# A graph layer on one core: where the norm roots run, when small loads and columns are made, and another order of the edge stage

## The chip, the core and the metric

The kernel runs on one core of a Trainium2 chip. The metric is device time in microseconds (us) of one execution. Five engines work side by side, each on its own in-order list of instructions: TensorE (PE, matrix products), VectorE (DVE), ScalarE (ACT), GpSimd (POOL, which here also issues the indirect loads, called gathers) and SyncE (SP, which issues most of the other transfers). Where one needs another's result it waits on a semaphore.

## The reference: what is computed

625 nodes with 512 values each, 20625 edges (a source, a destination, one of four types and a weight; the last 625 are loops of a node to itself). Cut to what matters:

```python
h = relu(layernorm(x))
total = sum over r of (h[src] @ W_rel[r] + b_rel[r]) * where(edge_type == r, edge_weight, 0)
agg   = segment_sum(total, dst) / maximum(segment_sum(edge_weight, dst), 1)
h2    = h @ W_self + b_self + agg
x1    = layer_norm(h + h2, g1, b1)
ffn   = gelu(x1 @ W_ffn1 + b_ffn1) @ W_ffn2 + b_ffn2
out   = x + layer_norm(x1 + ffn, g2, b2)
```

All is float32. Every layer norm needs one reciprocal square root for each node: this is the "root" of the text.

## The kernel before, in words

The nodes stand in 5 blocks of 125, the edges in 162 tiles of 128. The work has two stages, and the order of the instructions of every engine is fixed when the program is written: in the first stage by the order of the Python lines, in the second by a planner.

**Table stage.** x is loaded by block (`load_x`) and normalised without its root: `x_stats` (L346, L348) takes the statistics, `pre_norm` subtracts the mean and cuts at zero on DVE (L336, L337) and has POOL make the root as a power of -0.5 (`rsqrt_pow`, L313). PE turns each block (L320). Then come 20 steps, for relation r = 0 to 3 and block i = 0 to 4: `table_rows(r, i)` multiplies block i by W_rel[r] (L367), ACT scales the rows by the root (L375), and SP writes them to a table in DRAM (L377); the last nine stay in SBUF as well. A step is four matmuls; the profile shows two steps, 8 matmuls, as 3.49 us where nothing disturbs them.

Between these steps the Python lines put the work that prepares the edges. It is a chain:
- `find_tiles` (L467 to L470, DVE) searches `first_of_tile`, a row with the first destination of each tile, that SP loads at L221; `rows_of_tiles` has POOL gather five rows of destinations (L463, `dst`).
- `find_windows` (L477 to L482, DVE) searches these, and POOL gathers five windows of edges (L463, `win`).
- `edge_columns` (L423 to L427, DVE) makes columns of all edges, from `ed`, with no part in the chain.
- `slot_weights` and `slot_fields` (L494 to L523, DVE) turn the windows to fields; PE turns the fields (`turn_fields`, L598).
- `slot_hots` (L615, L618, L621, DVE) makes one-hot vectors of a quarter of a block's slots (a unit); `slot_sums` (L632, PE) multiplies them into a PSUM bank, and `empty_sums` (L638, DVE) adds three parts of it up to `sums_w`. There are 12 units for the three "dense" blocks 0 to 2; the first six are made in the table stage, the others in the edge stage.
- `first_edges` gathers, for each of the two other blocks, the first edges (L556). `first_columns` (L562 to L574, 13 short DVE steps) makes columns of them, and is the planner's `first_ready`.

SP's loads stand in the program's order too: x, W_rel[0], `first_of_tile` (between x's third block and the fourth and fifth), the edges, W_rel[1], and, by `later_loads(r)` after each relation, W_rel[2] and [3], W_self, `rows` (six rows of 512 values, each broadcast to 128 partitions, 1.5 MB, L210) and the weights of the feed-forward part. `rows` holds b_self, g1, b1, g2, b2 and b_ffn2 in this order.

**Edge stage.** A class `Plan` simulates the engines with a cost for each step, a `lag` after which a result is taken as there, counts of buffers (8 gathered tiles `ms`, three chunks `tr`, four PSUM banks `ps` and single ones for sums), and a rank or level for choosing between steps that could start. The order that it finds is emitted as each engine's order; the simulation's times are not used otherwise. Its steps:
- For each block the self part: 8 matmuls (L387) and a DVE step to z (L391).
- Blocks 0 to 2 (dense): 20 chunks of table rows times `sums_w` (L1044). The nine kept tiles are read from SBUF, the eleven others loaded by two with a lag of 6.2 (`chunk_load`, L1039).
- Blocks 3 and 4 by edges: 69 gathers of table rows on POOL (L920, by threes, with a pair of short pauses L916 after every fourth) with a lag `LAND` of 3.0. In each of 23 units ACT scales the first tile (L926), DVE adds the two others (L944), and PE sums the unit into its nodes with a one-hot matrix (L952). For a unit that is `parted`, ACT and DVE split the rows in a high and a low half (L930, L934) and PE runs two short matmuls (L964, L965); for one that is not, PE runs a full float32 product (L967). Of each list of units the last three are not parted. `gather_first` (L974) and `add_first` (L970) add single edges that cross a boundary, four gathers in all.
- When a block's sums are complete, its first norm: statistics and mean on DVE (L669, L300, L303/L305), the root, `za` (L676), x1 (L680), z = x1 + b_ffn2 (L683). The root is eight short DVE steps (`rsqrt_steps`: L651, L652, then L657 and L658 three times); for block 4 it is POOL's power (L313).
- Feed-forward of the block: PE (L715), gelu on ACT (L719), PE (L733), DVE (L741); then the second norm in the same way (L744, L300, L305, the root, L751, L756) and the store (L782). The blocks go in the order 0, 1, 3, 2, 4. The last one runs in two parts, and its root is ACT's square root with one DVE correction.
- `shifted`: xs + b2 for each block on DVE (L908), when nothing more urgent is there.

```python
if engine == "PE":
    o.lag = max(lag, Plan.BEHIND)
o.after = [(a, a.us if order and a.engine == engine else a.us + (0.0 if a.engine == engine == "PE" else a.lag))
           for a in after if a is not None]
```

These lines say when a step may start in the plan: after every step that it needs, plus that step's lag; nothing for a PE step behind a PE step.

Of the kernel before, what the change touches and what calls it, by code (L numbers as in the profile page):

```python
# [16 lines left out]
P = 128  # L17
# [51 lines left out]
class Plan:  # L69
# [5 lines left out]
    BEHIND = 1.0  # L75

# [60 lines left out]
def gnn_layer(ctx, tc, x, edges, edge_groups, firsts, fourths, windows, w_self, w_rel, w_ffn1, w_ffn2, brel_in, rows_in, bf1_in, out, n_edges):  # L137
# [74 lines left out]

    first_of_tile = early.tile([P, NT], I32, name="first_of_tile")
# [26 lines left out]
    bself_bc, g1_bc, b1_bc, g2_bc, b2_bc, bf2_bc = (  # L240
        rows[:, i * D:(i + 1) * D] for i in range(6))
# [68 lines left out]
    def rsqrt_pow(t):  # L310

        v, y = t[:, 0:1], t[:, 1:2]
        nc.gpsimd.tensor_tensor(y, v, half, op=ALU.pow)  # L313
        return y
# [348 lines left out]

    def first_norm(zi, name, got, pool_pow=False):
# [40 lines left out]
    def feed_forward(x1T_b, box, members, name, halves=False):  # L705
# [15 lines left out]
        def down(i):  # L721
# [24 lines left out]
            def mean_():  # L746
                got["mean"], got["t"] = aggregate(got["st"][:n, :len(cols), :], f"y{name}_{i}")
# [25 lines left out]
            norm.append(("scaled", "DVE", 0.72, scaled, ["a", "r3", "x"]))  # L773
# [16 lines left out]
    LAND = 3.0  # L790
# [15 lines left out]
    with tc.manual_schedule(engines={PE, DVE, ACT, mybir.EngineType.Pool}):  # L806
# [86 lines left out]
    first_ready = op("DVE", 2.4, first_columns, rank=(0.3,), level=6)  # L893

# [10 lines left out]

    shifted = {}
    for n, b in enumerate(ep.order):
        shifted[b] = op("DVE", 0.69, lambda b=b: nc.vector.tensor_add(xs[:, b, :], xs[:, b, :], b2_bc),  # L908
                        after=[own[b]], rank=(0.9, n), level=7)
# [26 lines left out]
    def parted(k, units):  # L936
        return k % PARTED[1] < PARTED[0] and k + 3 < len(units)
# [47 lines left out]
    for bs, units_ in of_sum.items():  # L985
        m, k0 = None, 0
        for b in inner:
            if bs == ((b, b + 1) if b < inner[-1] else (b,)):
                for q in range(EG - 1):
                    g_last = op("POOL", GATHER, lambda b=b, q=q: gather_first(b, q, ms), after=[g_last, first_ready],  # L990
# [59 lines left out]
    def weights_of(d):  # L1050
        nonlocal h, e
        for i, (dd, u) in enumerate(units):
# [3 lines left out]
            free = m[OUTER[d - 2]] if d >= 2 and u == 0 else None  # L1056
            h = op("DVE", 2.9, lambda d=d, u=u, box=box: box.update(hots=slot_hots(d, u)), after=[h], take=["low"],
                   rank=(0.55, i), level=0.18)
            for q in range(UNIT // QT):
                mm = op("PE", 0.33, lambda d=d, u=u, q=q, box=box: box.update(p=slot_sums(d, u, q, *box["hots"], (ps, "ps"))),  # L1060
                        after=[h, e, free], take=["ps"], give=["low"] if q == UNIT // QT - 1 else [], lag=0.25,
                        rank=(2, 1 + 0.01 * i), level=0.55)
                e = op("DVE", 0.57, lambda d=d, u=u, q=q, box=box: empty_sums(d, u, q, box["p"]), after=[mm], give=["ps"],
# [231 lines left out]
```

## Time and profile before

| | |
|---|---|
| median of 3 runs | 275.99 us (274.05 to 277.57) |
| the profiled execution | 278.13 us |
| its span, first to last instruction | 276.3 us |
| granted TensorE clock, mean | 0.977 |
| stages in the profile | table stage to about 91 us, edge stage from there |
| transfers | 47.94 MB, mean 173 GB/s |

How to read the lines that follow in the prediction. A group line has the line in the code, engine, operation, output <- inputs, shapes and count; then busy us and mean ns of one, then the idle time of the engine just before these instructions and what ended it. A timeline line has start, length, engine, line and operation, and in brackets the idle time before and its releaser. A waits line names who waited for what: us in total, times, longest. A chain line belongs to the chain of work that ended last. PEclk is the granted clock in tenths for 40 equal slices of the span (6.9 us each), 9 being 90% or more. Ends of matmuls are modelled and overlap the next one's start. L numbers in this document are those of the kernel before, unless it is said otherwise.

### The profile page before, as it was taken

How to read it: one execution, taken by the hardware profiler on the slowest of the kernel's cores; microseconds unless marked ns; L12 is line 12 of the kernel's file. 1: busy time of each engine (PE TensorE's matmuls, PEld its weight loads, DVE VectorE, ACT ScalarE, POOL GpSimd, SP SyncE). 2: the span in 40 equal slices, each digit the busy share in tenths (PEclk: the TensorE clock that was granted, in tenths of full speed). 3: DMA queues.
4: the chain of work that ended last, by engine and by line, in shares of the span. 5: the costliest groups of instructions: out<-in, count | busy, mean ns of one | idle time of the engine just before them, and what ended most of it. 6: DMA issues, size and time to landing. Idle time of an engine off the chain costs nothing.

```text
span 276.3 us, 3214 instructions
## 1 busy us (share of the span) xinstructions
PE 254.9 (92%) x1047; PEld 142.6 (52%) x1047; DVE 190.6 (69%) x447; ACT 63.9 (23%) x122; POOL 103.5 (37%) x148
## 2 busy tenths in 40 slices
PE   7999994999999997997896997899999999999990
PEld 3444441454554543453442456755367659494960
DVE  5540517989996859987899797799974976060614
ACT  3231112011310203221321022333044204030320
POOL 6252330002200067767775867574767010000000
PEclk9999997799999999999999899999999999999998
DMA  6939859466312577589999996563689101010101
GB/s 226 313 125 320 302 184 370 184 188 242 94 61 64 155 216 202 161 248 297 278 316 296 278 284 193 129 177 89 182 240 314 47 1 39 0 37 0 38 4 41
DMA packets 19972, 47.94 MB, mean 173 GB/s; under 512 B 2351, under 2 KB 3065, under 8 KB 19824
## 3 DMA queue, kind: packets, MB, share of 16 engines
q1 hardware_dynamic: 13348, 27.54, 30.5%
q0 software_dynamic: 6304, 19.89, 24.6%
q10 hardware_dynamic: 300, 0.26, 0.3%
q8 instruction: 9, 0.15, 0.2%
q14 instruction: 11, 0.09, 0.1%
HBM read 41.29 MB, written 6.52 MB: 173 GB/s over the span
## 4 chain that ended last, share of the span: by engine, by line
PE 62%; DMA 12%; POOL 8%; issue 8%; DVE 6%; SPq 1%; ACT 0%; DVEq 0%; POOLq 0%
PE pt L367 14%; PE pu L715 13%; PE po L733 12%; PE acc L1044 12%; POOL ms L920 5%; DMA tr<-table 5%; PE bank L632 3%; DMA ms<-table,row_i 3%; DMA xs<-in_x_dram 3%; PE acc L967 3%; DMA win<-in_windows_dram,at_i 2%; POOL dst L463 2%; PE pz L387 1%; PE acc L965 1%; PE acc L964 1%
## 5 line engine op out<-in xcount | busy, mean ns | idle before, releaser
L920 POOL DMA_INDIRECT ms<-table,row_i x69 | 69.3, 1004 | 55.7 <-DMA tr<-table 27.1
L367 PE MATMUL pt<-wr,hT 128*128 128x512 f32 x160 | 74.3, 614 | 0.0
L367 PEld LDWEIGHTS pt<-wr,hT 128*128 128x128 f32 x160 | 30.4, 197 | 33.5 <-issue 32.9
L715 PEld LDWEIGHTS pu<-x1T,w_sb 128*128 128x128 f32 x320 | 37.5, 192 | 5.2 <-issue 5.1
L715 PE MATMUL pu<-x1T,w_sb 128*128 128x125 f32 x320 | 38.0, 275 | 1.1 <-issue 1.1
L1044 PE MATMUL acc<-tr,sums_w 126*128 126x512 f32 x66 | 33.1, 626 | 3.4 <-DMA tr<-table 2.6
L733 PE MATMUL po<-w_sb,gT 128*125 128x512 f32 (+2 forms) x96 | 36.0, 522 | 0.0
L638 DVE TENSOR_REDUCE sums_w<-bank 126x160 f32<-126x480 f32 x48 | 29.9, 649 | 7.5 <-PE bank L632 6.7
L944 DVE SCALAR_TENSOR_TENSOR ea<-ms,wgt_g,ea 128x512 f32<-128x512 f32 x38 | 27.9, 747 | 10.4 <-DMA ms<-table,row_i 4.1
L926 ACT ACTIVATE ea<-ms,ed 128x512 f32<-128x512 f32 x23 | 15.8, 690 | 56.7 <-DMA ms<-table,row_i 27.9
L375 ACT ACTIVATE m<-pt,rx 125x512 f32<-125x512 f32 x20 | 13.8, 688 | 56.8 <-PE pt L367 45.2
L632 PEld LDWEIGHTS <-low 128*128 128x128 bf16 x192 | 17.2, 147 | 18.1 <-issue 17.8
L719 ACT ACTIVATE gT<-pu,bf 128x125 f32<-128x125 f32 x40 | 14.6, 367 | 49.6 <-PE pu L715 44.8
L1044 PE MATMUL acc<-m,sums_w 126*128 126x512 f32 x54 | 25.3, 597 | 0.0
L733 PEld LDWEIGHTS po<-w_sb,gT 128*125 128x125 f32 x96 | 16.3, 188 | 14.2 <-issue 12.1
L741 DVE TENSOR_TENSOR y<-po,z 125x512 f32<-125x512 f32 (+2 forms) x6 | 3.6, 601 | 26.3 <-PE po L733 26.3
L1044 PEld LDWEIGHTS acc<-tr,sums_w 126*128 126x128 f32 x66 | 12.2, 198 | 14.9 <-issue 11.0
L632 PE MATMUL bank<-high,low 128*128 128x120 bf16 x192 | 17.5, 226 | 2.4 <-issue 1.3
L387 PE MATMUL pz<-ws_sb,hT 128*128 128x512 f32 x40 | 18.1, 596 | 0.0
L621 DVE TENSOR_TENSOR high<-eq,turned 128x640 bf16<-128x640 bf16 x36 | 15.5, 487 | 0.4
L615 DVE TENSOR_TENSOR low<-turned,grid 128x2000 bf16<-128x2000 bf16 x12 | 14.3, 1190 | 1.3 <-ACT turned L601 1.3
L1044 PEld LDWEIGHTS acc<-m,sums_w 126*128 126x128 f32 x54 | 9.7, 191 | 8.9 <-issue 8.8
(169 smaller groups left out, 232.3 us busy)
## 6 DMA issues: line engine op xcount, KB each, us to landing
tr<-table SPq DMA_DIRECT2D x15, 504.0 KB
table<-m SPq DMA_DIRECT2D x20, 250.0 KB
w_sb<-in_L_gnn_W_ffn_dram SPq DMA_DIRECT2D x2, 2048.0 KB
wr<-in_L_gnn_W_rel_dram SPq DMA_DIRECT2D x3, 1024.0 KB
rows<-in_rows_dram SPq DMA_DIRECT2D x1, 1536.0 KB
ms<-table,row_i POOLq DMA_INDIRECT x69
ws_sb<-in_L_gnn_W_self_dram SPq DMA_DIRECT2D x1, 1024.0 KB
out_dram<-y SPq DMA_DIRECT2D x4, 224.0 KB
```

The lines of the kernel that those rows point to most:

```text
L367: nc.tensor.matmul(p, hT[i][:, k, :], wr_sb[r][:, k, :], start=(k == 0), stop=(k == KD - 1))
L387: nc.tensor.matmul(p[0], hT[i][:, k, :], ws_sb[:, k, :], start=(k == 0), stop=(k == KD - 1))
L621: nc.vector.tensor_mul(high[:, :, a * 2 * NC:(a + 1) * 2 * NC, :], eq, pairs(2 + a))
L632: nc.tensor.matmul(p[:, i * W:(i + 1) * W], low[:, t // TB, :, t % TB], high[:, t // TP, :, t % TP], start=True, stop=True)
L638: nc.vector.tensor_reduce(sums_w[OUTER[d]][:NG + 1, :, n0:n0 + 2 * QT].rearrange("p c (t h) -> p t h c", h=2), p[:NG + 1, :QT * 3 * 2 * NC ...
L715: nc.tensor.matmul(pu[:, :nn], w1_sb[:, k, f * P:(f + 1) * P], x1T_b()[:, k, :nn], start=(k == 0), stop=(k == KD - 1))
L719: nc.scalar.activation(box["gT"][:, f, :nn], pus[f][:, :nn], AF.Gelu, bias=bf1[:, f:f + 1])
L733: nc.tensor.matmul(po[h][:n, :w], box["gT"][:, f, at], w2_sb[:, f, c], start=(f == 0), stop=(f == KF - 1))
L920: nc.gpsimd.indirect_dma_start(out=ms[j], out_offset=None, in_=table[:, :], in_offset=bass.IndirectOffsetOnAxis(ap=row_i[:, j:j + 1], axis=0))
L926: nc.scalar.activation(box["sum"], ms[j], AF.Copy, scale=wgt[:, j:j + 1])
L944: nc.vector.scalar_tensor_tensor(to, ms[j], wgt_g[:, k, q - 1:q], box["sum"], op0=ALU.mult, op1=ALU.add)
L1044: nc.tensor.matmul(acc[b,], sums_w[b][:NG + 1, c, :], kept[(b, c) if (b, c) in kept else c][:NG + 1], start=first, stop=last)
```

## The change

- Roots: `root_by_pool` makes the root as one power on POOL in all first norms (block 4 had it so) and in the second norms of all blocks but the last one in order: eight norms move. The root waits in the plan for its mean with a lag, has cost 0.6 and goes ahead of all other POOL steps that could start (level -1).
- Loads: `first_of_tile` is loaded before x's third block instead of after it. `rows` is loaded in three parts: b2 alone (256 KB) right after W_rel[1], the first four rows (1 MB) and the last (256 KB) where the whole was loaded.
- Table stage: in the step (0, 0), `find_tiles` comes between the norm of x's third block and the statistics of its fourth; the roots of the fourth and fifth block come between the gathers. The five additions of b2 (`shifted` of before) stand in step (1, 0) after `edge_columns`. `first_columns` stands in step (3, 2). `first_ready` and `shifted` are gone from the plan.
- Plan: a PE step that follows DVE or ACT is planned 1.5 later, a POOL step 0.8 later. `LAND` is 4.5, the lag of a chunk load 8.0. The last unit alone of each list is not parted (before: the last three): of the 23 units 20 are split instead of 15. Slot sums of a unit do not wait for the emptying of the sums before; all units of the third dense block wait for the end of the first one's sum (before: the first unit of it). Levels of some DVE steps change; the second dense block takes the kept tiles first as the others do.

The plan's order therefore changes throughout the edge stage. For each engine the number of instructions in the list goes from 651 to 654 on PE, from 490 to 428 on DVE, from 154 to 159 on ACT, from 146 to 156 on POOL and from 93 to 95 on SP. In the new order of PE, the slot sums of the last two units of the second dense block stand right after the start of the second self part, the first edge sum comes after some 25 us of PE work of the stage (before: some 15), and all slot sums of the third dense block come before the first feed-forward product.

```diff
     BEHIND = 1.0
+    AFTER = {"PE": 1.5, "POOL": 0.8}
...
-        o.after = [(a, a.us if order and a.engine == engine else a.us + (0.0 if a.engine == engine == "PE" else a.lag))
-                   for a in after if a is not None]
+        behind = Plan.AFTER.get(engine, 0.0)
+        o.after = [(a, a.us if order and a.engine == engine else a.us + (0.0 if a.engine == engine == "PE" else a.lag)
+                    + (behind if a.engine in ("DVE", "ACT") and a.engine != engine else 0.0)) for a in after if a is not None]
...
     load_wr(0, [(2, 4)])
+    nc.sync.dma_start(first_of_tile, bass.AP(tensor=firsts.tensor, offset=firsts.offset, ap=[[0, P], [1, NT]]))
     load_x(2, 3)
-    nc.sync.dma_start(first_of_tile, bass.AP(tensor=firsts.tensor, offset=firsts.offset, ap=[[0, P], [1, NT]]))
     load_x(3, NB)
     nc.sync.dma_start(ed, edges)
     load_wr(1)
+    load_rows(b2_bc, 4 * D, 5 * D)
...
-            load_rows(rows, 0, 6 * D)
+            load_rows(rows[:, :4 * D], 0, 4 * D)
+            load_rows(rows[:, 5 * D:], 5 * D, 6 * D)
...
+    def root_by_pool(box, first):
+        return [("r3", "POOL", 0.6, lambda: rsqrt_pow(box["t"]), [first])]
...
-        rs = [("r3", "POOL", 0.9, lambda: rsqrt_pow(got["t"]), ["mean"])] if pool_pow else \
-            rsqrt_steps(got, "mean")
+        rs = root_by_pool(got, "mean") if pool_pow else rsqrt_steps(got, "mean")
...
-            norm += [] if halves else rsqrt_steps(got, "mean")
+            if not halves:
+                norm += root_by_pool(got, "mean") if pool_pow else rsqrt_steps(got, "mean")
...
-    LAND = 3.0
+    LAND = 4.5
...
-                    next_norm(i + 2 if i == 0 else i + 3)
+                    if i == 0:
+                        nonlocal stats
+                        pre_norm(2, stats)
+                        find_tiles()
+                        stats = x_stats(3)
+                    else:
+                        next_norm(i + 3)
...
-                if r == 0 and i < 3:
-                    if i == 0:
-                        next_norm(3)
-                        find_tiles()
-                    rows_of_tiles(2 * i, min(2 * i + 2, NB))
+                if (r, i) == (0, 0):
+                    rows_of_tiles(0, 2)
+                    next_norm(3)
+                    rows_of_tiles(2, 4)
+                if (r, i) == (0, 1):
+                    rows_of_tiles(4, NB)
...
                     edge_columns()
+                    for n in range(NB):
+                        nc.vector.tensor_add(xs[:, n, :], xs[:, n, :], b2_bc)
...
+                if (r, i) == (3, 2):
+                    first_columns()
...
-    first_ready = op("DVE", 2.4, first_columns, rank=(0.3,), level=6)
...
-        return k % PARTED[1] < PARTED[0] and k + 3 < len(units)
+        return k % PARTED[1] < PARTED[0] and k + 1 < len(units)
...
-            free = m[OUTER[d - 2]] if d >= 2 and u == 0 else None
+            free = m[OUTER[d - 2]] if d >= 2 else None
...
-                        after=[h, e, free], take=["ps"], give=["low"] if q == UNIT // QT - 1 else [], lag=0.25,
+                        after=[h, free], take=["ps"], give=["low"] if q == UNIT // QT - 1 else [], lag=0.25,
...
-        order = (*stay, *range(NC - KEPT)) if d != 1 else (*range(NC - KEPT), *stay)
+        order = (*stay, *range(NC - KEPT))
...
-                ld = op("SP", 0.3, lambda b=b, c=c, n=n: chunk_load(b, c, n), after=[ld], take=["tr"], lag=6.2, order=True,
+                ld = op("SP", 0.3, lambda b=b, c=c, n=n: chunk_load(b, c, n), after=[ld], take=["tr"], lag=8.0, order=True,
...
-                            lag=1.0 if name == "x1" and b != inner[-1] else 0.08, take=["ow"] * (2 if name in ("a", "x1") else 0),
+                            lag=1.0 if name == "r3" else 0.08, take=["ow"] * (2 if name in ("a", "x1") else 0),
...
-                            rank=(0.4, b), level=None if name == "bias" else 0.05)
+                            rank=(0.4, b), level=None if name == "bias" else -1 if name == "r3" else 0.05)
```

More of the change, by code (lines that the diff above doesn't have):

```diff
@@ L211, in load_rows @@
                                       ap=[[0, P], [1, n1 - n0]]))
+    bself_bc, g1_bc, b1_bc, g2_bc, b2_bc, bf2_bc = (
+        rows[:, i * D:(i + 1) * D] for i in range(6))
     first_of_tile = early.tile([P, NT], I32, name="first_of_tile")
@@ L312, in rsqrt_pow @@
         v, y = t[:, 0:1], t[:, 1:2]
-        nc.gpsimd.tensor_tensor(y, v, half, op=ALU.pow)
+        nc.gpsimd.tensor_tensor(y, v, half[:t.shape[0]], op=ALU.pow)
         return y
@@ L703, in root_steps, with feed_forward @@
         return [("root", "ACT", 0.25, root, [first]), ("r3", "DVE", 0.55, improve, ["root", "a"])]
-    def feed_forward(x1T_b, box, members, name, halves=False):
+    def feed_forward(x1T_b, box, members, name, halves=False, pool_pow=False):
         cuts = (0, 3 * D // 4, D)
@@ L746, in mean_ @@
             def mean_():
-                got["mean"], got["t"] = aggregate(got["st"][:n, :len(cols), :], f"y{name}_{i}")
+                got["mean"], got["t"] = aggregate(got["st"][:n, :len(cols), :], f"y{name}_{i}",
+                                                       pool_pow and not halves)
             def centred():
@@ L904, in gnn_layer @@
         own[b] = op("DVE", 0.68, added, after=[s], give=["ps"], rank=(0.6,) if b in OUTER else None)
[L906 to L909, printed above, removed]
     acc = {}
@@ L989, in gnn_layer @@
                 for q in range(EG - 1):
-                    g_last = op("POOL", GATHER, lambda b=b, q=q: gather_first(b, q, ms), after=[g_last, first_ready],
+                    g_last = op("POOL", GATHER, lambda b=b, q=q: gather_first(b, q, ms), after=[g_last],
                                 take=["ms"], lag=LAND, order=True, rank=(0, n))
@@ L1082, in gnn_layer @@
             if i == 8:
-                t = op("PE", 0.1, lambda: total_outside(), after=[m[b], first_ready], take=["ps"], give=["ps"], lag=2.0, rank=(2, 2.085))
+                t = op("PE", 0.1, lambda: total_outside(), after=[m[b]], take=["ps"], give=["ps"], lag=2.0, rank=(2, 2.085))
             if i == 16:
@@ L1088, in gnn_layer @@
         adds[b].append(op("DVE", 0.72, lambda b=b: add_to(b, lambda: acc[b,], slice(0, P)),
-                          after=[m[b], own[b]], give=["one"], rank=(0.4,)))
+                          after=[m[b], own[b]], give=["one"], rank=(0.4,), level=0.06))
     turned = {}
@@ L1100, in gnn_layer @@
         got, dep = {}, adds[b]
-        steps = first_norm(z[:, b, :], b, got, pool_pow=(b == inner[-1]))
+        steps = first_norm(z[:, b, :], b, got, pool_pow=True)
         made = {}
@@ L1126, in new_gT @@
             box["gT"] = edge.tile([P, KF, P], F32, tag="gT", name=f"gT_{name}", bufs=GT)
-        ups, downs = feed_forward(lambda b=blocks[0]: x1T[b], box, members, blocks[0], halves=last)
+        ups, downs = feed_forward(lambda b=blocks[0]: x1T[b], box, members, blocks[0], halves=last, pool_pow=True)
         gel = []
@@ L1147, in gnn_layer @@
             made["z"] = sums_done[blocks[i]]
-            made["x"] = shifted[blocks[i]]
             for name, eng, us, fn, needs in norm:
                 made[name] = op(eng, us, fn, after=[made[a] for a in needs] + (turned_g2 if last and name == "mean" else []),
-                                level=0.15 if name[0] == "y" else None, take=["ow"] * (2 if name in ("y0", "a") else 0),
+                                lag=1.0 if eng == "POOL" else 0.08,
+                                level=0.15 if name[0] == "y" else -1 if eng == "POOL" else None, take=["ow"] * (2 if name in ("y0", "a") else 0),
                                 give=["ps"] if name[0] == "y" else ["ow"] * 4 if name == "stored" else [], rank=None)
```

10 lines of the change are left out of this document (4 added, 6 removed).

## The prediction

> **What bounds the kernel now.** I read the busy shares first, then the clock line, then the table by stages, the waits of TensorE (PE), the chain, and the timelines around the two places where PE stood.
>
> ```profile
> PE 254.9 (92%) x1047; PEld 142.6 (52%) x1047; DVE 190.6 (69%) x447; ACT 63.9 (23%) x122; POOL 103.5 (37%) x148
> PEclk9999997799999999999999899999999999999998
> ```
>
> PE is busy for 92% of the span and sets the end; time can be won only where PE idles, runs at a lower clock, or does work that can be had cheaper. The clock line dips in slices 7 and 8 (45 us) and slice 23 (152 us).
>
> ```profile
> 20.00:45.00 25.00, 22.38 (x54) 9.66 (x52) 7.99 (x28) 5.21 (x8) 7.52 (x8) 1.00 0.78 274
> 45.00:91.00 46.00, 44.97 (x192) 23.28 (x193) 39.50 (x94) 8.77 (x15) 3.06 (x9) 0.93 0.45 155
> 91.00:120.00 29.00, 27.36 (x93) 12.81 (x91) 25.20 (x54) 5.46 (x10) 17.59 (x21) 1.00 0.65 188
> 120.00:150.00 30.00, 25.38 (x89) 12.30 (x86) 25.50 (x51) 7.52 (x12) 21.11 (x30) 1.00 0.99 294
> 150.00:180.00 30.00, 26.74 (x135) 16.88 (x135) 24.62 (x48) 6.76 (x15) 20.78 (x27) 0.94 0.78 229
> 180.00:210.00 30.00, 30.00 (x110) 16.39 (x111) 27.23 (x58) 9.23 (x17) 20.54 (x27) 1.00 0.65 183
> 147.00:156.00 9.00, 6.42 (x16) 2.61 (x15) 6.68 (x13) 1.28 (x2) 5.29 (x7) 0.81 0.99 292
> ```
>
> The columns are stretch, length, busy PE, weight loads, DVE, ACT, POOL, then granted clock, DMA share and GB/s. Table stage (to 91): 2.6 idle before 45, then clock 0.93. Edge stage (from 91): PE idle 1.6, 4.6 and 3.3 in the three stretches to 180, nothing after. DVE is at 25 to 27 of 30 there: it is the second resource. DMA is at 0.99 in 120 to 150.
>
> ```profile
> PE acc L1044 <- DMA tr<-table: 2.6, 1, 2.6
> PE tf L598 <- DVE fields L516: 2.3, 1, 2.3
> PE acc L965 <- DVE el L934: 2.0, 2, 1.8
> PE bank L632 <- issue: 1.3, 1, 1.3
> ```
>
> ```profile
> 150.59 1.44 PE L1044 MATMUL acc<-tr,sums_w 126*128 126x512 f32 x2 [2.58 <-DMA tr<-table]
> ```
>
> These are single stalls, each named: fields that come late (table stage), a chunk of the table that comes late (at 150.59, where the clock dips), split halves and slot sums (edge stage).
>
> ```profile
> 38.50 3.60 PE L367 MATMUL pt<-wr,hT 128*128 128x512 f32 x8
> 47.00 9.63 PE pt L367 x16
> 57.38 3.49 PE pt L367 x8
> 74.21 0.28 PE tf L598 x5
> ```
>
> The table rows end at 42.10 and go on at 47.00. The five turns between cost 0.28 where nothing waits, so 4.6 is stall. Then 16 matmuls take 9.63 where 8 take 3.49 later: 2.65 lost to the clock. At stake there: 4.6 + 2.65 = 7.3.
>
> **Part A: table stage.** The fields wait for window rows, these for rows of tiles, these for the first-edge row.
>
> ```profile
> 15.30 0.60 PE L320 MATMUL tp_h<-ident,z 128*128 128x128 f32 x4
> 9.80 0.15 DVE L337 TENSOR_SCALAR rx<-mv_x 128x1 f32<-128x1 f32 x1
> 13.59 0.21 DVE L467 CAST ends<-first_of_tile 128x162 f32<-128x162 int32 x1
> 16.59 1.14 POOL L463 DMA_INDIRECT dst<-in_fourths_dram,at_i  x1 [3.10 <-DVE at_i L470]
> 22.32 0.95 POOL L463 DMA_INDIRECT dst<-in_fourths_dram,at_i  x1 [0.30 <-issue]
> 22.68 0.42 SPq L210 DMA_DIRECT2D rows<-in_rows_dram  x1
> 29.76 0.32 DVE L477 CAST ends<-dst 128x160 f32<-128x160 int32 x1 [13.02 <-DMA dst<-in_fourths_dram,at_i]
> 40.70 0.35 DVE L494 CAST ends<-win 128x192 f32<-128x192 int32 x1 [6.64 <-DMA win<-in_windows_dram,at_i]
> ```
>
> The search (L467) moves ahead of the statistics of x's fourth block, behind the norm of the third (L337, done at 9.95; taken as 10.4 with its load shifted by one 83 KB transfer): 3.2 earlier. The gathers start at about 13.4 instead of 16.59. The norm of x's fourth block now follows the search (10.4 + 2.7: the search lay between 13.59 and the gather at 16.59, 0.3 of it the start of the gather), so it is subtracted by some 14.5; PE turns that block at 15.30, so this stays hidden by 0.8. Between the gathers now stand two pre-norm roots (0.56 each, below), so the fifth gather ends at about 20.9 instead of 23.27: 2.4 earlier. It also ends ahead of the 1.5 MB rows load (22.68), which before ran beside the landing (23.27 to 29.76 is 6.5). Landing is put between 3.6 and 6.5 after that, 24.5 to 27.4 (6.5 as before; 3.6 as an estimate, a little over half of it, without the 1.5 MB beside it), 2.4 to 5.3 ahead of 29.76, and the windows as much ahead of 40.70. Fields follow 6.0 after the windows (40.70 to 46.72), so the stall of 4.6 leaves 0 to 2.2; I take 1.0, about the middle, and no half clock: -(3.6 + 2.65) = -6.3; ends -7.3 and -2.4 (2.2 idle, and the half clock stays).
>
> ```profile
> L908 DVE TENSOR_TENSOR xs<-xs,rows 128x512 f32<-128x512 f32 x5 | 3.3, 680 | 0.0
> L657 DVE SCALAR_TENSOR_TENSOR rs_z<-rs_z 128x1 f32<-128x1 f32 x12 | 2.5, 211 | 0.0
> L658 DVE SCALAR_TENSOR_TENSOR rs_z<-rs_z 128x1 f32<-128x1 f32 x12 | 2.0, 166 | 0.4
> L313 POOL TENSOR_TENSOR rx<-rx,half 128x1 f32<-128x1 f32 x5 | 2.8, 559 | 6.6 <-DVE rx L337 6.6
> 225.34 1.00 POOL L313 TENSOR_TENSOR rs_z<-rs_z,half 128x1 f32<-128x1 f32 x1 [11.83 <-DVE rs_z L303]
> 226.38 0.75 DVE L680 SCALAR_TENSOR_TENSOR x<-za,rs_z,rows 128x512 f32<-128x512 f32 x1 [0.47 <-POOL rs_z L313]
> ```
>
> The five additions of b2 (3.4) move into DVE's 6.64 wait for the windows: nothing; with windows at 35.4 a tail of them would stand in front, 0.4. They wait for the new 256 KB row load behind the second weight matrix; if that came after 35, fields and PE would wait behind it. First columns, 13 short DVE steps of about 0.18 (2.4), move to row (3,2), where DVE runs beside PE's gapless rows: I charge 0.5. SP issues two loads more, 0.4 each, off the path. A in sum: -5.8.
>
> **Part B: sums of edge groups.** Five more of the 23 units are split, so that their sum runs as two short matmuls.
>
> ```profile
> 214.65 0.86 PE acc L967 x2
> 201.18 0.23 PE acc L965
> L934 DVE TENSOR_TENSOR el<-ea,eh 128x512 fp32r<-128x512 f32 x15 | 10.1, 684 | 1.9 <-PE acc L965 1.4 <-ACT eh L930 0.4
> ```
>
> An unsplit sum takes 0.86, a split one 2 x 0.23 = 0.46: 5 x 0.40 = -2.0 on PE. For it ACT casts and DVE subtracts five times more (5 x 0.68 = 3.4 DVE). Ends: -2.0, or 0 where PE waits for the low half as it did for 2.0 above.
>
> **Part C: roots and the edge stage anew.** Eight norms hand their root to POOL. DVE loses per norm 3 x (0.211 + 0.166) and two steps of 0.15 (as L337), 1.43, eight times 11.4, besides 3.3 (b2) and 2.4 (columns) that have left the stage, and gains 3.4: about 13.7 of its work between 91 and 240 goes. PE is the bound there, so this counts only where PE waits for DVE. POOL gets eight roots of 0.56 to 1.00: 4.5 to 8 us, in its own order between gathers. The scaling after a root waited 0.47; eight such waits (3.8) lie on DVE, where the relief covers them.
>
> The one root beside DVE's centring took 1.00, the five others 0.56. [...]
>
> What PE loses between 91 and 180: 1.64 + 4.62 + 3.26 = 9.5 idle, and 9.00 x 0.19 = 1.7 by the clock after the late chunk: 11.2. The new layout assumes longer lags (loads 8.0 instead of 6.2, gathers 4.5 instead of 3.0, 1.5 more where PE follows DVE). Reading the new order of PE's instructions against these durations I find three new places.
>
> ```profile
> 92.46 1.19 DVE L615 TENSOR_TENSOR low<-turned,grid 128x2000 bf16<-128x2000 bf16 x1
> 94.09 1.29 DVE L621 TENSOR_TENSOR high<-eq,turned 128x640 bf16<-128x640 bf16 x3
> 97.83 1.61 POOL L920 DMA_INDIRECT ms<-table,row_i  x1 [27.11 <-DMA tr<-table]
> 128.66 1.19 POOL L920 DMA_INDIRECT ms<-table,row_i  x1 [0.44 <-ACT ea L926]
> L920 POOL DMA_INDIRECT ms<-table,row_i x69 | 69.3, 1004 | 55.7 <-DMA tr<-table 27.1 <-issue 16.7 <-ACT ea L926 4.4
> ```
>
> First, slot sums stand right behind the start of the second self part (self part: 3.49), while DVE needs 2.9 for each of two sets of hot vectors (92.46 to 95.38): 2 x 2.9 against 3.49 and part of the next self part leaves an estimated 1.4. Second, a row addition that needs the 21st gather stands on DVE ahead of the emptying of the third block's first sums. In before that gather is issued 128.66 - 97.83 = 30.8 behind the first, itself 7 into the stage, and with a landing of some 6 it is ready 44 us into the stage; PE wants the emptied bank about 2.5 sooner. Third, the last two sets of hot vectors, five split halves and their rows meet in one stretch of DVE: 2 x 2.9 + 5 x 0.7 against some 6.7 of PE work beside them: 2.6. Together 6.5, where 11.2 stood: C = -4.7. [...]
>
> On that: at 150 an idle stretch of 2.6 was followed by clock 0.81 over 9 us. [...]
>
> After 180 PE has no idle, and the last block's tail keeps its form: 0.
>
> **Sum.** -5.8 - 2.0 - 4.7 = -12.5. The profiled execution took 278.13 with a span of 276.3, 1.83 around the span, and 2.1 above the median of 275.99 (274.05 to 277.57). The span comes to 263.8, the time to 265.6 on that execution's basis and 263.5 against the median.
>
> **Rivals.** R1, the windows land as late as before: the landing of the tiles' rows (6.5) is DMA time, the DMA share of 0.78 in 20 to 45 stays, and the b2 load comes on top. Then A is +0.5 instead of -5.8: 269.8. For it speaks the 0.78; against it that the gathers pass ahead of the 1.5 MB load. R2, the new layout stalls as long as the old: C = 0, 268.2. For it: gathers, not lags, may set the pace (the 69 keep POOL busy for 69.3, and their number is unchanged). Doing nothing that it says, R1 and R2 together: 274.5. R3, slower: POOL's queue stops at each root. A root waits for its mean, and every gather behind it waits too; a root emitted before its mean is ready holds them, and PE then lacks rows. From 263.5 it takes 18 us of holds to pass 281.5: five roots ahead of the last gather at 3.7 each. The new order has about five there, and the one root of before stood 11.83 waiting for its mean. Against it: the layout puts the root only when the mean is planned to be ready, and DVE is relieved by 13.7. Its time is 282.
>
> **How the numbers follow.** Forecast 0.55 (263.5; its own range is 256, with A at -7.3 and C at -11.2 in full, to 266, with 1.7 of clock loss and a stall of 2.2 left in A); R1 0.13, R2 0.13, both 0.09, R3 0.10. A measurement of this kernel tells about 2% from no change: 270.5 to 281.5 counts as the same. The forecast, R2 and half of R1 (269.8 lies close to the bound) are faster: 0.55 + 0.13 + 0.06 = 0.74; the other half of R1 and both together within 2%: 0.16; R3 slower: 0.10. The range from 256 to 271 leaves out both together and R3, 0.19.
>
> **What would show it.** A: the turns of the fields wait no more than 2.2 at 42 to 45, clock 1.00 in slices 7 and 8, windows at 35 to 38; wrong if DVE's wait for windows still ends at 40. B: three unsplit sums at 0.86, twenty split. C: PE's idle between 90 and 180 at 6 to 7 in three waits of 1.4 to 2.6 (slot sums on DVE or on a bank), no wait for a chunk over 1. Roots: POOL 0.56 to 1.00 each, gathers behind them not over 1 late. The prediction fails if POOL's waits for a mean exceed 3 and split sums wait behind them, or if DVE, not PE, has no idle in 120 to 180.

## The result, and the profile after

| | before | after |
|---|---|---|
| median | 275.02 us (273.74 to 277.57, 4 runs) | 263.71 us (262.54 to 266.27, 4 runs) |
| ratio | | 0.959, 95% interval 0.948 to 0.970 |
| profiled execution, span | 278.13, 276.3 | 264.32, 262.4 |
| start of the first self part (end of the table stage) | 91.05 | 89.32 |
| from there to the end of the span | 185.3 | 173.1 |

The change makes the kernel faster by 4.1%; forecast were 263.5. The two profiled spans differ by 13.9, of which 1.7 lie in the table stage and 12.2 in the edge stage. The ratios leave out executions more than 1.5% above the fastest of the same kernel; of run 4 below that leaves two of ten (267.32 and 269.49), while the other eight took 273.19 to 275.08. Line numbers of the changed kernel are higher by about 5 in the table stage and by 7 to 13 behind it.

The page after, busy shares and the clock line:

```profile
PE 248.7 (95%) x1047; PEld 141.6 (54%) x1047; DVE 184.4 (70%) x388; ACT 66.4 (25%) x127; POOL 112.2 (43%) x156
PEclk9999999999999999999999999999999999999997
```

PE is busy for 6.2 less and idle for 7.7 less (21.4 before, 13.7 now). The two dips of the clock line are gone. The table by stages after (stretch, length, then busy PE, PEld, DVE, ACT, POOL, clock, DMA share, GB/s):

```profile
20.00:45.00 25.00, 23.89 (x63) 10.75 (x62) 12.60 (x36) 4.71 (x7) 7.09 (x8) 1.00 0.66 225
45.00:86.00 41.00, 38.36 (x170) 20.21 (x170) 37.17 (x97) 8.81 (x15) 3.07 (x9) 1.00 0.55 193
86.00:115.00 29.00, 28.64 (x108) 13.63 (x106) 27.87 (x52) 5.61 (x10) 15.31 (x19) 1.00 0.64 182
115.00:145.00 30.00, 29.23 (x103) 14.77 (x103) 21.57 (x36) 6.59 (x11) 22.23 (x28) 1.00 0.86 260
145.00:175.00 30.00, 29.21 (x137) 17.78 (x136) 26.39 (x45) 8.22 (x16) 20.76 (x26) 1.00 0.84 235
```

Read the idle time of PE as length less the first number. Between 86 and 175 it is 0.36 + 0.77 + 0.79 = 1.92, where the same stages had 9.5 before. In the table stage it is 1.1 + 2.6, where it was 2.6 + 1.0: the idle time moved, it did not go. PE's waits after:

```profile
PE bank L637 <- DVE sums_w L643: 3.9, 7, 2.5
PE tf L603 <- DVE fields L527: 0.6, 1, 0.6
PE acc L978 <- DVE el L947: 0.4, 2, 0.2
PE tf L603 <- DVE fields L528: 0.4, 1, 0.4
```

No chunk is waited for any more, and the feed-forward for 0.2 at most. The fields cost 1.0 instead of 3.5, but one wait of 2.5 for slot sums is new. Where it comes from, by the timelines of DVE, ACT and PE after:

```profile
27.96 0.32 DVE L482 CAST ends<-dst 128x160 f32<-128x160 int32 x1 [10.36 <-DMA dst<-in_fourths_dram,at_i]
38.73 0.35 DVE L499 CAST ends<-win 128x192 f32<-128x192 int32 x1 [3.41 <-DMA win<-in_windows_dram,at_i]
47.76 1.20 DVE L620 TENSOR_TENSOR low<-turned,grid 128x2000 bf16<-128x2000 bf16 x1 [3.07 <-ACT turned L606]
```
```profile
42.65 0.69 ACT L380 ACTIVATE m<-pt,rx 125x512 f32<-125x512 f32 x1 [4.88 <-DMA table<-m]
46.23 0.69 ACT L380 ACTIVATE m<-pt,rx 125x512 f32<-125x512 f32 x1 [2.89 <-DMA table<-m]
46.82 0.84 ACT L606 COPY turned<-tf 64x320 bf16<-64x320 bf16 x2
```
```profile
44.75 0.23 PE L603 MATMUL tf<-ident_b,fields 128*128 128x128 bf16 x1 [0.36 <-DVE fields L528]
58.92 0.41 PE L637 MATMUL bank<-high,low 128*128 128x120 bf16 x4 [2.48 <-DVE sums_w L643]
```

The windows are there at 38.73 instead of 40.70, and PE has turned the fields at 44.98. But ACT's copies of them stand in ACT's order behind a scaling, and that waits for a buffer whose row is still being written to the table. So the hot vectors start at 47.76, where they started at 47.99 before, and PE, which came 2 earlier and at full clock, waits at 56.43 for what it had met in time before.

### The profile page after: what moved, and what is told of

Its sections match the earlier page's. It is cut to its first block, busy times and chain, and to the rows that moved or that the text cites. A ratio compares the mean times of both kernels' runs of the same rounds, so it can differ in the third digit from the quotient of the medians.

```text
span 262.4 us, 3165 instructions
## 1 busy us (share of the span) xinstructions
PE 248.7 (95%) x1047; PEld 141.6 (54%) x1047; DVE 184.4 (70%) x388; ACT 66.4 (25%) x127; POOL 112.2 (43%) x156
## 4 chain that ended last, share of the span: by engine, by line
PE 61%; DVE 23%; DMA 9%; issue 2%; ACT 2%; SPq 1%; DVEq 0%; ACTq 0%
PE pt L372 17%; PE pu L722 14%; PE po L740 13%; PE acc L1057 9%; DVE sums_w L643 5%; DMA table<-m 5%; DVE high L626 4%; DVE low L620 3%; DMA ms<-table,row_i 3%; DVE ea L957 3%; PE bank L637 2%; PE acc L978 1%; DVE eq L623 1%; PE acc L977 1%; SPq L212 1%
## 5 line engine op out<-in xcount | busy, mean ns | idle before, releaser
L933 POOL DMA_INDIRECT ms<-table,row_i x69 | 72.1, 1046 | 52.1 <-DMA tr<-table 26.5
L372 PE MATMUL pt<-wr,hT 128*128 128x512 f32 x160 | 72.0, 599 | 0.0
L372 PEld LDWEIGHTS pt<-wr,hT 128*128 128x128 f32 x160 | 29.7, 193 | 32.0 <-issue 31.1
L957 DVE SCALAR_TENSOR_TENSOR ea<-ms,wgt_g,ea 128x512 f32<-128x512 f32 x43 | 31.8, 750 | 8.0 <-DMA ms<-table,row_i 7.6
L1057 PE MATMUL acc<-tr,sums_w 126*128 126x512 f32 x66 | 30.7, 596 | 0.0
L643 DVE TENSOR_REDUCE sums_w<-bank 126x160 f32<-126x480 f32 x48 | 28.7, 651 | 0.8 <-PE bank L637 0.8
L380 ACT ACTIVATE m<-pt,rx 125x512 f32<-125x512 f32 x20 | 13.8, 688 | 57.8 <-PE pt L372 46.4
L637 PEld LDWEIGHTS <-low 128*128 128x128 bf16 x192 | 15.8, 146 | 15.3 <-issue 15.1
L947 DVE TENSOR_TENSOR el<-ea,eh 128x512 fp32r<-128x512 f32 x20 | 13.6, 685 | 11.1 <-ACT eh L943 11.1
L637 PE MATMUL bank<-high,low 128*128 128x120 bf16 x192 | 15.9, 224 | 3.9 <-DVE sums_w L643 3.9
L943 ACT CAST eh<-ea 128x512 fp32r<-128x512 f32 x20 | 11.7, 584 | 27.3 <-DVE ea L957 24.4
```

What stands on the lines that cost most here:

```text
L372: nc.tensor.matmul(p, hT[i][:, k, :], wr_sb[r][:, k, :], start=(k == 0), stop=(k == KD - 1))
L637: nc.tensor.matmul(p[:, i * W:(i + 1) * W], low[:, t // TB, :, t % TB], high[:, t // TP, :, t % TP], start=True, stop=True)
L643: nc.vector.tensor_reduce(sums_w[OUTER[d]][:NG + 1, :, n0:n0 + 2 * QT].rearrange("p c (t h) -> p t h c", h=2), p[:NG + 1, :QT * 3 * 2 * NC ...
L933: nc.gpsimd.indirect_dma_start(out=ms[j], out_offset=None, in_=table[:, :], in_offset=bass.IndirectOffsetOnAxis(ap=row_i[:, j:j + 1], axis=0))
L957: nc.vector.scalar_tensor_tensor(to, ms[j], wgt_g[:, k, q - 1:q], box["sum"], op0=ALU.mult, op1=ALU.add)
L1057: nc.tensor.matmul(acc[b,], sums_w[b][:NG + 1, c, :], kept[(b, c) if (b, c) in kept else c][:NG + 1], start=first, stop=last)
```

## The experiments

All ratios are to the kernel before, run on the same chip beside it. The changed kernel's own is 0.959 (0.948 to 0.970). Differences "against the changed kernel" are of the medians, or of the ratios times 275. The runs were made on different chips, on which the median of the kernel before lay between 274.33 and 278.95, so the ratios are the safer ones. The numbers are those of the labels; none has the number 11.

**1. The search alone.** The kernel before with the load of `first_of_tile`, `find_tiles` and its gathers as in the change.

```diff
+    nc.sync.dma_start(first_of_tile, bass.AP(tensor=firsts.tensor, offset=firsts.offset, ap=[[0, P], [1, NT]]))
     load_x(2, 3)
-    nc.sync.dma_start(first_of_tile, bass.AP(tensor=firsts.tensor, offset=firsts.offset, ap=[[0, P], [1, NT]]))
...
+                        pre_norm(2, stats)
+                        find_tiles()
+                        stats = x_stats(3)
...
+                    rows_of_tiles(0, 2)
+                    next_norm(3)
+                    rows_of_tiles(2, 4)
```

> The kernel before with nothing but the earlier search: its row loaded ahead of x's third block, the search behind that block's norm, the gathers as in the changed kernel. Theory 1 (from the two traces): the windows come about 2 earlier, the half clock after the stall mostly goes, but the one-hot vectors start hardly earlier because ACT's turned copies stand behind a scaling that waits for a buffer; so -1 to -3.5 against before, about 273 on a day when before takes 275. Theory 2 (the prediction's part A): -6.3 without the columns, about 269.

Ratio 0.995 (0.987 to 1.002), not told from no change. In its trace the self part starts at 87.55, 3.5 earlier than in the trace of before, but the stage behind it takes 187.5 instead of 185.3, with chunks waited for by 5.4 instead of 2.6. Theory 2, my part A, is refuted.

**2. The change without the search.** The reverse edit in the changed kernel.

> The changed kernel with the search, its row's load and its gathers where they were before; the rest stays changed. Theory 1: the fields' stall and the half clock come back, +1 to +4 against the changed kernel, about 265 to 268 where before takes 275. Theory 2: +6.3, about 270. A third way: 0, if the edge stage starts when the hot vectors are ready and these stay where they are.

264.25 us, ratio 0.957 (0.945 to 0.970): the third way, no difference. Its search starts at 13.71, as before, and yet the rows of tiles are there at 27.74 and the windows at 38.27, earlier than with the early search (27.96 and 38.73). The landing does not follow the start of the gathers: over all traces here the rows of tiles are there at 27.32 to 28.84 with the early search and at 27.36 to 29.76 with the late one.

**3. Five buffers for the scaled rows.** In the changed kernel:

```diff
-            m = early.tile([P, D], F32, tag="msg", name=f"m_{c}", bufs=3)
+            m = early.tile([P, D], F32, tag="msg", name=f"m_{c}", bufs=5)
```

> The changed kernel with five instead of three buffers for the scaled table rows. Theory 1: ACT's wait of 11.5 for a written row goes, its copies of the turned fields run when the fields are turned (45 instead of 47), the hot vectors start about 2 earlier and PE's 2.5 wait for their sums at 56 shrinks to 0.5 or less: -2 against the changed kernel, about 261.5 where before takes 275. Rival: DVE is full from 45 to 58 whatever ACT does, and the wait stays: 0.

262.94 us, ratio 0.952 (0.941 to 0.964); the median is 0.8 lower than the changed kernel's, and the intervals overlap almost wholly. The mechanism is there, for the hot vectors start at 45.70 and the wait is 0.7:

```profile
44.74 0.85 ACT L606 COPY turned<-tf 64x320 bf16<-64x320 bf16 x2 [0.43 <-PE tf L603]
56.85 0.41 PE L637 MATMUL bank<-high,low 128*128 128x120 bf16 x4 [0.70 <-DVE sums_w L643]
```

But without more buffers runs 2 and 6 too had the hot vectors early (45.50 in run 2). The wait of 2.5 is there in some executions and not in others: of the seven traces that have three buffers and the early search of the changed kernel, the profile after and run 7 have it (there the hot vectors start at 47.98 and PE waits 2.7), the five others start the hot vectors at 45.07 to 46.61.

**4. Roots on DVE, laid out again.** In the changed kernel the eight roots are `rsqrt_steps` once more, and the planner finds its own order.

```diff
-        steps = first_norm(z[:, b, :], b, got, pool_pow=True)
+        steps = first_norm(z[:, b, :], b, got, pool_pow=(b == inner[-1]))
...
-        ups, downs = feed_forward(lambda b=blocks[0]: x1T[b], box, members, blocks[0], halves=last, pool_pow=True)
+        ups, downs = feed_forward(lambda b=blocks[0]: x1T[b], box, members, blocks[0], halves=last)
```

> The changed kernel with the eight norm roots as DVE steps again, laid out anew by the same planner. If the layout gave the edge stage its gain (my theory): +0 to +2 against the changed kernel, as DVE has 7 of 30 idle between 115 and 145 and PE hardly waits for it. Rival: the relief of DVE by 11.4 gave it: +5 or more, with PE waiting for split halves and slot sums again.

Ratio 0.974 (0.963 to 0.984), about +4 against the changed kernel, between the two theories. The ratio rests on two of ten executions, and the median of all ten, 273.76, is 10 above the changed kernel's, so this run does not decide between them.

**5. Pool roots alone.** The kernel before with the eight roots on POOL, and with the cost, lag and level that the change gives a root in the plan.

```diff
-        steps = first_norm(z[:, b, :], b, got, pool_pow=(b == inner[-1]))
+        steps = first_norm(z[:, b, :], b, got, pool_pow=True)
...
+            if not halves:
+                norm += root_by_pool(got, "mean") if pool_pow else rsqrt_steps(got, "mean")
```

> The kernel before with the eight roots on POOL (a root planned at 0.6 and ahead of other POOL steps), everything else of the change left out; the planner lays the edge stage out again. Theory 1 (the relief of DVE by 11.4 frees gather buffers sooner and is what the edge stage gained): -6 to -9 against before. Theory 2 (the new lags and levels gave it, the roots only together with them): 0 to -3. Theory 3 (roots stop the queue of gathers): slower than before.

278.75 us, ratio 1.0125 (1.005 to 1.020): a little slower. DVE's busy time falls from 190.6 to 180.5, and yet PE's waits in the edge stage add up to 11.7, where they were 9.5 before. The longest:

```profile
PE acc L970 <- DVE es L947: 2.5, 2, 1.9
PE acc L970 <- DVE z L982: 2.1, 1, 2.1
PE acc L968 <- DVE el L937: 2.0, 2, 1.7
PE bank L632 <- DVE z L391: 1.7, 1, 1.7
```

10 us less of work on DVE bring nothing under the old lags. Theory 1 is refuted in its strong form.

**6. The changed order, roots' arithmetic on DVE.** The order stays; at each root's place DVE runs the eight short steps.

```diff
-        return [("r3", "POOL", 0.6, lambda: rsqrt_pow(box["t"]), [first])]
+        def steps():
+            for _, _, _, fn, _ in rsqrt_steps(box, first):
+                fn()
+
+        return [("r3", "POOL", 0.6, steps, [first])]
...
```

> The changed kernel with its order of instructions kept, but the eight roots (and that of block 4) worked by DVE's short steps at the same places of the order. Theory 1: DVE's 1.4 for each root lands on row additions and slot sums, gathers wait for buffers, and it takes +6 to +9 against the changed kernel, as the re-laid version with DVE roots did (about 270 to 273). Theory 2 (the order decides): +0 to +3, about 264 to 267.

266.99 us, ratio 0.968 (0.963 to 0.974): 3.3 over the changed kernel by the medians, 2.5 by the ratios, at the edge of what theory 2 said. So much is, by the medians, the worth of the eight roots, and one more that is block 4's, for DVE in this order; the intervals of the two ratios overlap.

**7. The old lags.** The changed kernel with `AFTER = {}`, `LAND = 3.0` and 6.2 for a chunk.

> The changed kernel with the three lags as before (nothing added behind DVE or ACT, gathers 3.0, chunk loads 6.2), laid out again. Theory 1 (relief of DVE): +0 to +3 against the changed kernel. Theory 2 (the lags): +6 or more, with a chunk load waited for by 2 to 3 as before.

294.54 us, ratio 1.066 (1.059 to 1.074): +31 against the changed kernel by the medians, +29 by the ratios. Theory 2's "+6 or more" covers that, but not by the wait that it named: PE waits for no chunk in this trace. POOL's timeline in this run:

```profile
206.17 0.96 POOL L933 DMA_INDIRECT ms<-table,row_i  x1 [0.30 <-issue]
...
212.75 0.99 POOL L318 TENSOR_TENSOR rs_y<-rs_y,half 125x1 f32<-125x1 f32 x1 [5.02 <-DVE rs_y L308]
226.76 1.01 POOL L318 TENSOR_TENSOR rs_y<-rs_y,half 125x1 f32<-125x1 f32 x1 [13.01 <-DVE rs_y L308]
240.77 1.08 POOL L318 TENSOR_TENSOR rs_y<-rs_y,half 125x1 f32<-125x1 f32 x1 [13.01 <-DVE rs_y L308]
244.66 1.38 POOL L933 DMA_INDIRECT ms<-table,row_i  x1 [2.81 <-DVE z L983]
```

Gathers stop from 207 to 245. Three roots stand in between, but the gather behind them still waits 2.8 for an addition of single edges (L983) that frees its buffer. That addition needs the self part of block 4, which the planner ranks as a filler, and which stands in PE's order behind three feed-forwards:

```profile
238.66 3.60 PE L392 MATMUL pz<-ws_sb,hT 128*128 128x512 f32 x8
```

Run 12 tests this.

**8. Three units unsplit.** The changed kernel with `k + 3 < len(units)`.

> The changed kernel with the last three units of each list unsplit, as before (15 instead of 20 split). By the prediction's part B: +2.0 on PE (8 unsplit sums instead of 3), less if DVE's 3.4 fewer of subtraction free gathers: +1 to +2. Rival: the split costs as much on DVE as it saves on PE: 0 or a gain.

265.58 us, ratio 0.963 (0.958 to 0.969): +1.9 by the medians, 1.2 by the ratios, with intervals that overlap. The trace bears it out: PE is busy for 249.9, where the three traces of the changed kernel's edge stage with its split (after, runs 2 and 3) have 248.1 to 248.7.

**9. The lags alone.** The kernel before with `AFTER`, `LAND = 4.5` and 8.0.

> The kernel before with the three longer lags alone (1.5 and 0.8 behind DVE and ACT, gathers 4.5, chunk loads 8.0), roots on DVE, laid out again. Theory L (the lags by themselves give an order that fits the chip): -4 to -8 against before. Theory M (lags and roots only pay together, as each alone has done little: the pool roots alone +1.2%, the new layout with DVE roots -2.6%): 0 to -3.

296.33 us, ratio 1.076 (1.061 to 1.091): both theories miss, it is slower by some 20. DVE's waits in this run:

```profile
DVE y L743 <- PE po L735: 22.2, 5, 11.7
DVE z L981 <- PE acc L1046: 19.0, 1, 19.0
```

One addition of a block's sum (L981) stands in DVE's order for 19.0 while that sum is not ready.

**10. Without the lag behind DVE and ACT.** The changed kernel with `AFTER = {}` alone.

> The changed kernel without the added lags behind DVE and ACT; gathers 4.5 and chunk loads 8.0 stay. In its order the last self part stays early (some 20 us of PE work into the edge stage). If the loss of 31 without all three lags came from the self part that went behind three feed-forwards, this one costs little: +0 to +4 against the changed kernel. If the lag behind DVE is what fits the order to the chip: +10 or more.

270.1 us, ratio 0.976 (0.961 to 0.991): +4.6 by the ratios (+6.4 by the medians), just past the +4 of the first case and short of the second; the interval overlaps that of the changed kernel.

**12. Old lags, self part early.** Run 7 with

```diff
-        rank = (2, 0.1 * n) if n < len(OUTER) else (5, n)
+        rank = (2, 0.1 * n)
```

> The changed kernel with all three old lags, as in the run that took 294.5, but the self parts of the two inner blocks ranked early like the others (their sums in the third block's place instead of 77 us of PE work later). If the late self part (the gathers of single edges hold buffers until it is done, POOL stands from 208 to 245) made that loss: 265 to 272. If the lags themselves did: over 285.

270.47 us, ratio 0.978 (0.968 to 0.988): 24 of the 31 are back. The late self part made most of run 7's loss; the short lags themselves cost about 5 by the ratios, as in run 10.

**13. Lags and the planner's other edits.** Run 9 with the levels 0.07 and 0.06, `free` for all units, `after=[h, free]` for the slot sums and the kept tiles first; roots, b2, columns, split and table stage as before.

> The kernel before with the three longer lags and with the planner's other edits (levels of two DVE steps, slot sums that don't wait for the emptying before, all units of the third block behind the first block's sum, kept tiles first), but with roots and columns on DVE in the edge stage, fewer split sums and the old table stage. The lags alone took +7.6%. If these edits are what makes the lags pay: -1 to -3% against before, like the changed kernel with its roots on DVE (-2.6%). If it takes the relief of DVE: slower than before, +3% or more.

265.5 us, ratio 0.968 (0.962 to 0.975): the first case, and by more than it said. PE's waits:

```profile
PE bank L634 <- DVE z L393: 1.7, 2, 1.4
PE bank L634 <- DVE sums_w L640: 1.6, 5, 0.7
```

With the old work on DVE (busy for 189.7, before 190.6), these edits and the lags take PE's waits in the edge stage from 9.5 down to 2.7; 0.85 of the waits for `sums_w` shown lies in the table stage. This is three quarters of the whole change's gain (3.15 of 4.1%). The roots, the columns, b2, the split and the search together would add the rest, 0.95%, which is not told from nothing, as the intervals overlap.

## Why the prediction was right, and where it was right by luck

The time was foretold to 0.2, and that closeness is luck. The forecast was 12.5 below a median of 275.99, and the measured drop is 11.3 from a median of 275.02. Two of its terms were wrong, each by some 3 to 6, in opposite directions.

**Part A, forecast -5.8, measured about 0.** The pair of traces shows -1.7 (91.05 to 89.32); the experiments show that not even that belongs to the change. With the table stage unchanged, the first self part started at 91.05 in the profile of before, at 88.62 in run 5, 87.12 in run 9 and 87.00 in run 13. In the same order the rows of tiles were there at 29.76, 28.92, 27.51 and 27.36, so the later they landed, the later the stage ended. With the changed one it started at 89.32 after, and between 86.62 (run 4) and 90.77 (run 7) in the seven other traces. Run 13, whose table stage is that of before, beside the trace of before (first line):

```profile
91.05 5.37 PE L387 MATMUL pz<-ws_sb,hT 128*128 128x512 f32 x12
87.00 5.37 PE L389 MATMUL pz<-ws_sb,hT 128*128 128x512 f32 x12
27.36 0.32 DVE L479 CAST ends<-dst 128x160 f32<-128x160 int32 x1 [10.86 <-DMA dst<-in_fourths_dram,at_i]
PE tf L600 <- DVE fields L524: 0.6, 1, 0.6
PE tf L600 <- DVE fields L525: 0.4, 1, 0.4
```

Run 13 has the same two waits as the changed kernel and no half clock (1.00 over 45 to 87.4, where the trace of before has 0.50 over 46.4 to 51.4). The step that failed is "At stake there: 4.6 + 2.65 = 7.3": it took a stall of the one profiled execution, which was 2.1 above the median, for a stall of the kernel. Rival R1's premise, that the landing is a matter of the DMA and not of the gathers' start, held (run 2). Its price did not, since two of the four traces of the old table stage have no such stall to keep, and run 5 a smaller one. In the smaller steps the search started 1.7 earlier, not 3.2, as x's third block itself was there at 10.46 instead of 8.46 with a load put ahead of it and more behind.

**Part B, forecast -2.0, measured -1.2 to -1.9** (run 8, by the ratios and by the medians; the difference alone is within the noise, and PE's busy time, 1.2 to 1.8 more without the split, bears it out). The size is as forecast or a little less. Waits for split halves are 0.4 in all.

**Part C, forecast -4.7, in the traces -8 to -10.** 185.3 to 173.1 is 12.2, less 2.0 for the split. Two other traces of the same order, those of runs 2 and 3, have 175.4 and 174.6 in place of 173.1. The old stalls went as the step said, and the lost clock with them. The term that was mis-sized is the 6.5 of new stalls. The three places were found, with these sizes after: at the slot sums behind the second self part 0.36 instead of 1.4, at the third block's first sums 0.32 instead of 2.5, in the stretch around 151 0.8 instead of 2.6:

```profile
97.16 0.41 PE L637 MATMUL bank<-high,low 128*128 128x120 bf16 x4 [0.20 <-DVE sums_w L643]
133.54 0.41 PE L637 MATMUL bank<-high,low 128*128 128x120 bf16 x4 [0.32 <-DVE sums_w L643]
151.01 0.41 PE L637 MATMUL bank<-high,low 128*128 128x120 bf16 x4 [0.47 <-DVE sums_w L643]
```

The second of them depends on the execution. In run 2, whose edge stage is in the same order, PE waited 3.11 there, and the granted clock was 0.69 and then 0.75 in the two stretches of 3 us behind it. DVE stood for a gather's landing, with the emptying of the sums behind that row addition, which is the mechanism that the prediction named:

```profile
131.00 0.76 DVE L950 SCALAR_TENSOR_TENSOR ea<-ms,wgt_g,ea 128x512 f32<-128x512 f32 x1 [2.47 <-DMA ms<-table,row_i]
132.32 0.65 DVE L643 TENSOR_REDUCE sums_w<-bank 126x160 f32<-126x480 f32 x1
133.02 0.41 PE L637 MATMUL bank<-high,low 128*128 128x120 bf16 x4 [3.11 <-issue]
```

So this term was a stall that can come, at about its size and with the lost clock that the prediction put at 1.7, and the profile after is an execution without it. The 263.5 itself takes nothing for the clock behind these stalls (the 1.7 is in the range alone); that was the author's estimate, and run 2's 0.69 and 0.75 speak against it. Each of the three was worked out as a straight sum of DVE's durations against PE's, with gathers as late as before. That is argued, not shown, to be the cause of the excess. The relief of DVE, which was counted at nothing, is worth 2.5 to 3.3 in this order (run 6, within the noise by the ratios) and nothing under the old lags, where the planner found another order (run 5).

**Roots.** Forecast 4.5 to 8 on POOL; measured 6.9 for nine, block 4's among them. They are of two kinds:

```profile
L318 POOL TENSOR_TENSOR rs_y<-rs_y,half 125x1 f32<-125x1 f32 x4 | 3.6, 910 | 18.6 <-DVE rs_y L308 18.6
L318 POOL TENSOR_TENSOR rs_z<-rs_z,half 128x1 f32<-128x1 f32 x5 | 3.3, 663 | 9.2 <-DVE rs_z L308 9.1
197.20 0.58 POOL L318 TENSOR_TENSOR rs_y<-rs_y,half 125x1 f32<-125x1 f32 x1
212.10 0.96 POOL L933 DMA_INDIRECT ms<-table,row_i  x1 [0.16 <-issue]
214.12 0.99 POOL L318 TENSOR_TENSOR rs_y<-rs_y,half 125x1 f32<-125x1 f32 x1 [1.05 <-DVE rs_y L308]
```

The four of 0.99 to 1.08 started when their mean came and ran beside DVE's centring (L684 or L759, 0.74 or 0.75 each); the five of 0.57 or 0.58 came later in POOL's queue, when DVE had gone on to other work: the one at 166.12 took 0.58 beside a subtraction for a split half (L947, 0.68 from 166.16). So the upper end of the forecast, 1.00 for each of the eight, did not come: in this trace a root's time went with what DVE did beside it, and a root that is late in the queue misses the centring.

**R3, the slower case, did not come.** POOL waited 27.7 for means, more than the 18 that the rival needed. But the last gather was issued at 212.10, and the first root that waited stands behind it, at 214.12. In run 7 the roots do stand between gathers, over a gap of 37; there the buffer, not the root, ended last, so that R3's mechanism alone was not seen at work. Run 5, slower by 1.25%, has pool roots under the old lags. There too the last gather (208.01) was issued before the first root that waited in the edge stage (218.97), so R3 is not its cause; what is stays open.

**R2** was half right: the lags alone do not remove stalls (run 9), and moving them back costs 31, 24 of it by way of one misplaced self part (runs 7 and 12). What removes the stalls is the order that lags and levels give together (run 13). Which of the levels and conditions of run 13 does it stays open; they were not tried one by one.

## What to carry to other kernels

Before a stall in one profile is priced, look whether it is there in more than one execution: here 7.3 of a table stage were there in one trace and, with rows that landed 2.4 earlier, gone in another of the same stage. Under a list scheduler an edit's worth is not additive: of this change the search alone gave 0.5%, not told from nothing, the pool roots alone cost 1.25%, the lags alone cost 7.6%, and the lags with four small rules gave 3.15%. So price the order that comes out, above all where fillers and additions of late sums stand in an in-order queue, and not the edits that went in.

## What the runs showed of the hardware

An idle stretch of 2.48 on PE (56.43 to 58.92 after) left the granted clock at 1.00 in its stretch and over the next 3 us, where one of 2.58 in the trace of before, which ended at 150.59, was followed by 0.68 over the next 5.4 us (0.81 over 147 to 156). In the trace of run 1 an idle stretch of 2.44 that ended at 142.39 was followed by 0.70 over the next 2.6 us, and one of 2.49 that ended at 172.20 by 1.00 over the next 2.8 us. A shorter one was followed by a lower clock and a longer one was not, so the length alone does not decide; what else does was not shown.

With the same table stage, the rows of tiles were there at 29.76 in the trace of before, where the last of the five gathers ended at 23.27, and at 27.36 in that of run 13. A write of 250 KB to the table kept its buffer for up to 12.7 us (the chain of the profile after):

```profile
33.47 12.66 DMA table<-m
```
